# Turned token rows in DRAM: one array with 512 columns a block of features for each slot, in place of two halves of 256

## The chip, the cores and the metric

The kernel runs on one core of one Trainium2 chip. The metric is the device time of one execution in microseconds. A core has the engines TensorE (PE in the profile; its weight loads are PEld), VectorE (DVE), ScalarE (ACT), GpSimd (POOL) and SyncE (SP), and 16 DMA engines that serve the DMA queues of SP (q1 in the profile) and of POOL (q0).

## What is computed

Four batches of 1024 tokens with 1024 features go through a cross attention and a mixture of experts. Cut to what matters here:

```python
x = x + xattn(layernorm(x), ctx, Wq, bq, Wk, bk)      # x + teacher_logits @ softmax(q k^T)^T
xt = layernorm(x).reshape(4096, 1024)
scores = sigmoid(xt @ gate_w.T)
_, sel = top_k(scores + expert_bias, 2)               # 2 of 8 experts a token
order = argsort(sel.reshape(-1))                      # 8192 (token, expert) pairs, by expert
tok_idx = order // 2
routed_in = xt[tok_idx] * scores_sorted[:, None]
h = silu(ragged_dot(routed_in, w1t)) * ragged_dot(routed_in, w3t)   # hidden 704, bf16
routed_out = ragged_dot(h, w2t)
shared = (silu(xt @ sw1.T) * (xt @ sw3.T)) @ sw2.T    # float32, for every token
out = x + shared.at[tok_idx].add(routed_out)
```

## The kernel before

The work has three stages, and TensorE's order is written out by hand through all of them.

**Attention and routing** (to about 640 us). Tokens go through in tiles of 128. For each token tile the kernel also finds its two experts, scales its row by the two scores in bf16, and scatters the scaled rows (with the token's number behind the 1024 features) into a DRAM list `xrows`, one region an expert.

**Shared experts, and the turning of rows** (about 640 to 1473 us). Eight shared slots of 512 tokens in float32. A shared slot `s` is `up(s)` (L937: six blocks of products, the last five of them by a scheme of seven products over `xb`, `xs` and the weights) and two `down_pair` (L1033). `block(s + 1)` (L154) loads the next slot's 2 MB `xb` on SP's queue once the products of `up(s)` have read it; GpSimd makes the four sums `xs` of it (`differences`, L174); `residuals` (L996) loads the rows that `down_pair` adds to and stores. In slots 0 to 3 `convert` (L244) writes one more expert's weights as bf16 on POOL's queue.

In the same stage the generator `turns()` (L1001) prepares the first `NTURN` = 15 of the `NS` = 23 expert slots. An expert slot has 512 rows of one expert, in four quarters of 128. One step of the generator stands for one quarter: GpSimd gathers rows of a later quarter (`ask`, L1006, into one of four `xg` buffers), VectorE reads the token numbers from the gathered rows (L1022), SP turns the quarter with a DMA transpose into half of a tile `xh` (L1027; two such tiles), and after every second quarter SP stores `xh`, 128 partitions x 8 blocks of features x 256 columns, to DRAM (L1019, the last one L1031). `up(s)` calls the generator twice for each of its five blocks from s = 2 on (L974), so the steps are tied to TensorE's progress through the engines' program order. SP works its list in order: transposes, stores, `xb`, residuals and outputs stand in one queue.

**Expert slots** (1473 us to the end). For each of 23 slots (L1176) TensorE does 88 products (L131, `upwards`: 11 groups of 8 with weights `w13` stationary and the turned rows `xTb` moving; only as many columns as the slot has rows, 32 to 512), then the products of `w2` (L1161 to L1169). A slot's rows come from `fetch_turned(s)` (L906) for the first 15 slots and from `fetch_rows` (L882) with TensorE transposes for the rest; its weights come from gathers on POOL's queue, `fetch_up` (L888, `w13`, 22.5 KB a partition) and `fetch_down` (L897, `w2` with 10 KB a partition, and `w2t`). `w13` and `w2` are not fetched again where the expert stays the same two slots on. All of these have two buffers, by the slot's parity. When the 88 products of slot `s` are done, SP may issue `fetch_turned(s + 2)` (L1192) and GpSimd `fetch_up(s + 2)`; then come the four adds of slot `s`'s results into `out` (L1208, POOL's queue, DMAs that add in DRAM; GpSimd takes them in program order) and `fetch_down(s + 2)`. `fetch_turned(0)` and its weights are issued in the last shared slot (L1117), `fetch_turned(1)` after it (L1173).

The layout that the change touches is this: each slot's turned rows lie in DRAM as two tiles of [128, 8, 256] bf16, one for each half of 256 columns.

```python
xturned = [[dram.tile([P, KC, 2 * P], BF16, name=f"xturned_{i}_{h}") for h in range(2)]
           for i in range(NTURN)]
```

So a store writes 4 KB in one piece for each partition, and the load of a half, whose target `xTb` is [128, 8, 512], puts pieces of 256 columns (512 bytes) with gaps of as much between them.

Of the kernel before, what the change touches and what calls it, by code (L numbers as in the profile page):

```python
# [33 lines left out]
BF16 = mybir.dt.bfloat16  # L34
# [7 lines left out]
P = 128  # L42
# [6 lines left out]
KC = D // P  # L49
# [7 lines left out]
SLOT = 512  # L57
# [6 lines left out]
NTURN = 15  # L64
# [15 lines left out]
def xattn_moe_kernel(ctx: ExitStack, tc: tile.TileContext, x, ctxT, wqT, wkT, bqk, gwT, ebias,  # L80
                     w13, w2, w2t, sw13, sw2, sw2t, consts, out):
    nc = tc.nc

    dram = ctx.enter_context(tc.tile_pool(name="dram", bufs=1, space=DRAM))
# [10 lines left out]
    def const(k):  # L95
# [13 lines left out]
    width = cp.tile([P, NS, 1 + NQ], I32, name="width")  # L109
    beyond = cp.tile([P, NS, NQ], I32, name="beyond")  # L110
    tokens_of = [cp.tile([P, NQ], I32, name=f"toks_{i}") for i in range(NTURN)]
    xturned = [[dram.tile([P, KC, 2 * P], BF16, name=f"xturned_{i}_{h}") for h in range(2)]
               for i in range(NTURN)]


    places = bass_types.dram_disjoint_views(xrows, 2 * NT)
# [112 lines left out]
    with ExitStack() as a:  # L229
# [317 lines left out]
        with tc.manual_schedule(engines=vector_scalar):  # L547
# [37 lines left out]
            for p in range(NT // 2):  # L585
                g = 2 * p
                b, i = divmod(g, LT)
# [161 lines left out]
    def gather(dst, src, idx, **bound):  # L749
        nc.gpsimd.indirect_dma_start(out=dst, out_offset=None, in_=src,  # L750
                                     in_offset=bass.IndirectOffsetOnAxis(ap=idx, axis=0), **bound)
# [128 lines left out]
    weights, fetched, slots = [], {}, {}  # L880
# [22 lines left out]
    def xT_of(s):  # L903
        return bps[s % 2].tile([P, KC, SLOT], BF16, tag="xT", name=f"xTb_{s}")

    def fetch_turned(s):  # L906
        slots[s] = xT_of(s), tokens_of[s]
        for h in range(2):
            nc.sync.dma_start(slots[s][0][:, :, h * 2 * P : (h + 1) * 2 * P], xturned[s][h])

    def turned_rows(s, q):
        if q == 0:
# [19 lines left out]
    with shared, tc.manual_schedule(engines=vector_scalar | {mybir.EngineType.SP}):  # L932
# [68 lines left out]
        def turns():  # L1001

            blocks = list(itertools.product(range(NTURN), range(NQ)))
            asked = []

            def ask(s, q):  # L1006
                xg = tr.tile([P, ROW], BF16, tag="xg", name=f"xgt_{s}_{q}", bufs=4)
                gather(xg.bitcast(I32), xrows, li[:, s, q : q + 1])
                asked.append(xg)

            for b in blocks[:2]:
                ask(*b)
            yield
            done = None
            for j, (s, q) in enumerate(blocks):
                if j + 2 < len(blocks):
                    ask(*blocks[j + 2])
                if done:
                    nc.sync.dma_start(*done)  # L1019
                    done = None  # L1020
                xg = asked.pop(0)
                nc.vector.tensor_tensor(tokens_of[s][:, q : q + 1], xg[:, D : D + 2].bitcast(I32),  # L1022
                                        beyond[:, s, q : q + 1], ALU.bitwise_or)
                h, v = divmod(q, 2)
                if v == 0:
                    xh = tr.tile([P, KC, 2 * P], BF16, tag="xh", name=f"xh_{s}_{h}", bufs=2)
                nc.sync.dma_start_transpose(xh[:, :, v * P : (v + 1) * P], xg[:, :D])  # L1027
                if v:
                    done = xturned[s][h], xh
                yield  # L1030
            nc.sync.dma_start(*done)  # L1031

# [63 lines left out]
        tb = ExitStack()  # L1096
        table = tables(pool(tb, "tb", 1, "right"))
        turning = turns()
        residuals(0)
        for s in range(NJ):  # L1100
# [10 lines left out]
            if s + 1 == NJ:  # L1111
                for _ in turning:
                    pass
                tb.close()
                sums.close()
                bps.append(pool(ctx, "b0", 1, "right"))
                fetch_turned(0)  # L1117
                fetch_up(0)
                fetch_down(0)
                nextparts = list(widths(0))  # L1120
            else:
                block(s + 1)
# [48 lines left out]

    outs, adds = bass_types.dram_disjoint_views(out, NQ), []
    fetch_turned(1)  # L1173
    fetch_up(1)
    fetch_down(1)
    for s in range(NS):  # L1176
# [14 lines left out]
        if s + 2 < NTURN:  # L1191
            fetch_turned(s + 2)  # L1192
# [110 lines left out]
```

## Time and profile before

| | |
|---|---|
| Median of 3 runs | 2016.29 us (2012.39 to 2018.24) |
| The profiled execution's own time | 2016.26 us |
| Its span in the profile | 2014.5 us, mean granted TensorE clock 0.992 |
| Busy: PE, PEld, DVE, ACT, POOL | 97%, 58%, 41%, 26%, 32% |
| DMA moved | 340.37 MB in 179972 packets, mean 169 GB/s |
| POOL's queue q0, SP's queue q1 | 43024 packets, 172.78 MB; 136832 packets, 166.04 MB |
| Stores of turned rows (L1019, L1031) | 30, 512 KB each |
| Loads of turned rows (L909) | 30, 512 KB each |

Of a group of instructions the profile gives the line, engine, operation, names (target <- sources) and count, then the busy time and the mean ns of one, then the time that the engine idled before them and what ended most of that. A chain of waits is read in order of time: start, length, what ran or was waited for. A row of a table by stretches has the stretch and its length, then busy time (and instructions) of PE, PEld, DVE, ACT and POOL, the granted TensorE clock (1.00 is full), the share of the 16 DMA engines' time that packets took, and GB/s. A row of DMA queues has packets, MB and the share of the 16 engines' time in the stretch asked for. SPq means SP's DMA queue, where issues are seen.

### The profile page before, as it was taken

What the parts mean: (1) busy time and instruction counts of PE and PEld (TensorE: products, weight loads), DVE (VectorE), ACT (ScalarE), POOL (GpSimd) and SP (SyncE); (2) the same over time, 40 slices, a digit from 0 to 9 for tenths busy, and PEclk for the clock granted to TensorE, in tenths of its full rate; (3) what the DMA queues carried; (4) which work ended last, traced back from release to release, by engine and by line L of the source; (5) the groups of instructions that cost most, each with busy time, mean ns of one, the idle gap of its engine ahead of it and who ended that gap; (6) DMA issues with size and microseconds to landing.
All of it is one profiled execution on the core that took longest, in us unless ns stands there. A gap on an engine that the chain in (4) does not pass through costs nothing.

```text
span 2014.5 us, 24206 instructions
## 1 busy us (share of the span) xinstructions
PE 1961.7 (97%) x8992; PEld 1175.0 (58%) x9107; DVE 828.2 (41%) x2014; ACT 514.6 (26%) x900; POOL 650.2 (32%) x598
## 2 busy tenths in 40 slices
PE   8999999999999999999999999999999897999997
PEld 5555655655454448485858576767655553456665
DVE  5456566556863426313131313231333332224353
ACT  3344444454432101010101010101022232223232
POOL 0423433433642140312121212121124533256563
PEclk9999999999999999999999999999999998999999
DMA  4263473373765143595959272727646877489994
GB/s 122 85 172 116 150 197 117 119 209 135 243 204 210 64 114 98 149 221 138 211 141 239 84 204 80 194 90 188 237 99 127 247 194 226 102 216 334 297 306 81
DMA packets 179972, 340.37 MB, mean 169 GB/s; under 512 B 80400, under 2 KB 119824, under 8 KB 176016
## 3 DMA queue, kind: packets, MB, share of 16 engines
q0 software_dynamic: 43024, 172.78, 32.8%
q1 hardware_dynamic: 136832, 166.04, 27.0%
q8 instruction: 73, 1.20, 0.2%
q14 instruction: 43, 0.35, 0.1%
HBM read 280.80 MB, written 166.20 MB: 222 GB/s over the span
## 4 chain that ended last, share of the span: by engine, by line
PE 93%; DMA 3%; DVE 1%; issue 1%; ACT 0%; another core or an unknown queue 0%; POOL 0%; POOLq 0%; SPq 0%; DVEq 0%; ACTq 0%
PE pa L131 22%; PE bank L131 15%; PE pc L131 12%; PE bank L1169 6%; PE qa L131 6%; PE pb L131 6%; PE pu L131 4%; DMA xTb<-xturned 3%; PE pq L310 3%; PE qc L131 3%; PE pe L322 3%; PE pt_c L131 2%; PE pt_a L258 1%; PE qb L131 1%; PE pt_t L258 1%; PE pt_x L258 1%
## 5 line engine op out<-in xcount | busy, mean ns | idle before, releaser
L131 PE MATMUL bank<-xTb,w 128*128 128x0 bf16 x2024 | 318.9, 318 | 18.0 <-DMA xTb<-xturned 15.5
L131 PEld LDWEIGHTS <-w 128*128 128x128 bf16 x2024 | 190.8, 99 | 128.6 <-issue 22.7
L750 POOL DMA_INDIRECT xgt<-xrows,li x60 | 57.3, 955 | 431.8 <-DMA xh<-xgt 173.3
L1208 POOL DMA_INDIRECT out_dram<-yt,toks x92 | 146.7, 1595 | 115.7 <-DVE yt L1204 81.9
L1169 PE MATMUL bank<-w,hTb 128*128 128x0 bf16 x920 | 165.6, 327 | 3.1 <-DVE hTb L148 3.1
L275 POOL TENSOR_TENSOR rs<-ve,con 128x1 f32<-128x1 f32 x64 | 47.7, 745 | 321.7 <-DVE ve L273 318.0
L148 DVE TENSOR_TENSOR hTb<-sg_b,bank 128x512 bf16<-128x512 f32 x115 | 78.7, 687 | 162.7 <-PE bank L131 149.0
L131 PE MATMUL pa<-xs,sw_sb 128*128 128x256 f32 x560 | 132.3, 379 | 0.0
L1169 PEld LDWEIGHTS <-hTb 128*128 128x128 bf16 x920 | 72.2, 98 | 92.4 <-issue 13.7
L131 PE MATMUL pa<-aT,xT 128*128 128x512 f32 x256 | 116.8, 599 | 1.6 <-DVE x L412 1.4
L147 ACT ACTIVATE sg_b<-bank 128x512 f32<-128x512 f32 x115 | 68.4, 597 | 184.7 <-PE bank L131 158.7
L131 PEld LDWEIGHTS pa<-xs,sw_sb 128*128 128x128 f32 x560 | 106.4, 190 | 14.4
L1204 DVE COPY yt<-bank 128x512 f32<-128x512 f32 x92 | 61.6, 689 | 120.8 <-PE bank L1169 112.4
L1206 ACT COPY yt<-bank 128x512 f32<-128x512 f32 x92 | 53.5, 585 | 147.9 <-PE bank L1169 136.0
L964 DVE TENSOR_TENSOR one<-one,pb 128x256 f32<-128x256 f32 x35 | 14.7, 420 | 172.4 <-PE pb L131 172.4
L528 POOL DMA_INDIRECT xrows<-rr,toi x64 | 64.6, 1009 | 61.9 <-issue 40.1
L412 DVE SCALAR_TENSOR_TENSOR x<-pa,rs,x 128x512 f32<-128x512 f32 x64 | 47.8, 748 | 86.6 <-PE pa L131 80.6
L168 ACT ACTIVATE st_c<-pt_c 64x256 f32<-64x256 f32 x7 | 2.6, 377 | 311.8 <-PE pt_c L131 311.8
L1055 DVE TENSOR_TENSOR x2c<-x2c,qa 128x512 f32<-128x512 f32 x64 | 43.8, 685 | 93.5 <-PE qa L131 93.5
L268 DVE BATCH_NORM_STATS2 st<-x 128x6 f32<-128x512 f32 x128 | 81.8, 681 | 0.6
L750 POOL DMA_INDIRECT w<-w13b,wi x23 | 23.2, 1009 | 180.5 <-PE bank L131 152.7
L131 PE MATMUL pu<-xb,sw_sb 128*128 128x512 f32 x176 | 76.3, 594 | 0.9 <-PE pt_t L258 0.9
(268 smaller groups left out, 3445.0 us busy)
## 6 DMA issues: line engine op xcount, KB each, us to landing
w13b<-in_w_dram POOLq DMA_DIRECT2D x8, 2816.0 KB
x<-in_x_dram SPq DMA_DIRECT2D x32, 512.0 KB
x2d<-x SPq DMA_DIRECT2D x32, 512.0 KB
xtd<-xtT SPq DMA_DIRECT2D x32, 512.0 KB
xb<-xtd SPq DMA_DIRECT2D x8, 2048.0 KB
x2c<-x2d SPq DMA_DIRECT2D x16, 1024.0 KB
out_dram<-x2c SPq DMA_DIRECT2D x16, 1024.0 KB
xturned<-xh SPq DMA_DIRECT2D x30, 512.0 KB
```

Of the source, the lines that this page charges most:

```text
L131: nc.tensor.matmul(part(pp), w(c), part(xT(c)), start=start and c == 0, stop=c == blocks - 1, skip_group_check=not start)
L147: nc.scalar.activation(sg, pa, AF.Silu)
L148: nc.vector.tensor_tensor(hT[:, f, :], sg, pb, ALU.mult)
L258: nc.tensor.transpose(pt[:, j, :], src[:, c * P : (c + 1) * P], ident)
L268: nc.vector.bn_stats(st[:, h, :], src[:, h * 512 : (h + 1) * 512])
L310: nc.tensor.matmul(pq[:, i, j, :], w[c // CH][:, c % CH, :], ct[c // CH][:, c % CH, :], start=c == 0, stop=c == CC - 1)
L322: nc.tensor.matmul(pe[:, h, :], qs[b][:, m * P : (m + 1) * P], ks[b][:, h * 512 : (h + 1) * 512], start=True, stop=True)
L528: nc.gpsimd.indirect_dma_start(out=places[2 * (g + i) + k], out_offset=bass.IndirectOffsetOnAxis(ap=tois[k][:, i : i + 1], axis=0), in_=rr ...
L750: nc.gpsimd.indirect_dma_start(out=dst, out_offset=None, in_=src, in_offset=bass.IndirectOffsetOnAxis(ap=idx, axis=0), **bound)
L1169: nc.tensor.matmul(part(py), hT[:, f, toks], part(w[:, f, cols]), start=False, stop=f == NF - 1, skip_group_check=q < 2)
L1204: nc.vector.tensor_copy(yt[:, q, h * 512 : (h + 1) * 512], py)
L1208: adds.append([nc.gpsimd.indirect_dma_start(out=outs[q], out_offset=bass.IndirectOffsetOnAxis(ap=toks[:, q : q + 1], axis=0), in_=yt[:, q, ...
```

## The change

The two halves of a slot lie in one DRAM array, [128, 8, 512] bf16. A store still takes one tile `xh` of 256 columns, and its 256 columns of each block of features now lie as 512 bytes, with 512 bytes of the other half between them. The load of a slot is one DMA of 1 MB, with 8 KB in one piece for each partition on both sides, in place of two of 512 KB. The transposes, the gathers, the buffers in SBUF and their number, and what TensorE, VectorE, ScalarE and GpSimd do stay as they are.

```diff
-    xturned = [[dram.tile([P, KC, 2 * P], BF16, name=f"xturned_{i}_{h}") for h in range(2)]
-               for i in range(NTURN)]
+    xturned = [dram.tile([P, KC, SLOT], BF16, name=f"xturned_{i}") for i in range(NTURN)]
...
     def fetch_turned(s):
         slots[s] = xT_of(s), tokens_of[s]
-        for h in range(2):
-            nc.sync.dma_start(slots[s][0][:, :, h * 2 * P : (h + 1) * 2 * P], xturned[s][h])
+        nc.sync.dma_start(slots[s][0], xturned[s])
...
                 nc.sync.dma_start_transpose(xh[:, :, v * P : (v + 1) * P], xg[:, :D])
                 if v:
-                    done = xturned[s][h], xh
+                    done = xturned[s][:, :, h * 2 * P : (h + 1) * 2 * P], xh
                 yield
             nc.sync.dma_start(*done)
```

## The prediction

> **What bounds the kernel now.** I read the page first, then the waits of TensorE, then the chain, then what the DMA engines did inside the two stretches that the chain names. The page says that TensorE is the bound nearly everywhere, and its costliest group shows the one place where it is not:
>
> ```profile
> PE 1961.7 (97%) x8992; PEld 1175.0 (58%) x9107; DVE 828.2 (41%) x2014; ACT 514.6 (26%) x900; POOL 650.2 (32%) x598
> ...
> L131 PE MATMUL bank<-xTb,w 128*128 128x0 bf16 x2024 | 318.9, 318 | 18.0 <-DMA xTb<-xturned 15.5
> ```
>
> Of the 18.0 us that TensorE sat idle before the expert stage's first products, 15.5 ended when a load of turned rows landed. TensorE's waits between 1470 and 1820 us say how often:
>
> ```profile
> PE bank L131 <- DMA xTb<-xturned: 15.5, 2, 10.0
> ```
>
> Twice, once for 10.0 us. The chain (start, length, what) shows where; the timeline of TensorE gives the idle time in brackets:
>
> ```profile
> 1562.40 14.32 PE bank L131 x88
> ...
> 1577.30 30.70 DMA xTb<-xturned
> 1607.99 0.14 issue
> 1608.13 16.98 PE bank L131 x88
> ...
> 1632.95 14.32 PE bank L131 x88
> ...
> 1647.85 30.41 DMA xTb<-xturned
> 1678.26 0.14 issue
> 1678.40 20.69 PE bank L131 x88
> ```
>
> ```profile
> 1608.13 16.98 PE L131 MATMUL bank<-xTb,w 128*128 128x0 bf16 x88 [5.54 <-DMA xTb<-xturned]
> ```
>
> ```profile
> 1678.40 20.69 PE L131 MATMUL bank<-xTb,w 128*128 128x0 bf16 x88 [10.01 <-DMA xTb<-xturned]
> ```
>
> Counting the blocks of 88 from 1473.6 us, these are slots 6 and 9. Each follows a nearly empty slot (5 and 8), whose 88 products took 10.35 and 7.47 us, so less time than usual lay between issue and use. A load of 1 MB takes some 31 us here; beside a quiet POOL queue its 2048 packets pass in 4 us (1489.5 to 1493.5). Look also at the granted clock (the 0.50 or 1.00 behind POOL's column):
>
> ```profile
> 1608.00:1610.00 2.00, 1.87 (x6) 0.89 (x7) 0.00 (x0) 0.00 (x0) 1.69 (x3) 0.50 1.03 207
> 1614.00:1616.00 2.00, 2.00 (x14) 1.18 (x13) 0.69 (x1) 0.04 (x1) 0.00 (x0) 1.00 1.06 417
> 1678.00:1680.00 2.00, 1.60 (x4) 0.59 (x5) 0.00 (x0) 0.00 (x0) 1.06 (x2) 0.50 1.03 213
> ```
>
> After each wait TensorE runs at half clock for some microseconds. That is why slot 6's block took 16.98 us where slots 4 and 7 took 14.32, and slot 9's 20.69 where slots 10 to 12 took 18.99.
>
> Why is the load slow? The DMA view from 1582 to 1586 us, when expert weights (POOL's queue q0) and turned rows (SP's queue q1) are both waiting:
>
> ```profile
> q0 software_dynamic: 64, 1.44, 92.2%
> q1 hardware_dynamic: 64, 0.03, 2.7%
> ```
>
> Equal packet counts: the engines take one packet from each queue in turn. A weight packet is 1.44 MB / 64 = 22.5 KB and takes 0.922 x 64 us / 64 = 0.92 us; a packet of turned rows is 512 bytes and takes 27 ns. The load has 128 packets an engine, and each waits for one of q0's.
>
> **The change, part by part.** *The load.* Two DMAs of 1024 runs of 512 bytes become one DMA of 128 runs of 8 KB, or 8 packets an engine. From weight packets (0.92 us for 22.5 KB) or from the 4 KB rows of the stores (983.9 to 985.5 us: 0.864 x 25.6 us / 122 = 0.18 us) an 8 KB packet costs about 0.34 us, so 8 cost 2.7 us. Slot 6's load starts moving at 1578.1 and weights follow at 1579.9, so some five packets pass first and three wait for one of q0's each (3 x 0.92). It lands near 1584 us. Were each run cut into 4 KB pieces, some ten would wait, and it lands near 1591. TensorE wants it at 1602.4. Slot 9's load starts at 1648.6 and is wanted at 1668.4: the same sum gives 1654, or 1661. Both waits go.
>
> *What each is worth.* Slot 6: 5.54 idle + (16.98 - 14.32) half clock = 8.20 us. Slot 9: 10.01 + (20.69 - 18.99) = 11.71 us. Together 19.9 us.
>
> *What is late next.* For slot 6, the w13 packets end at 1588.0, 14 us early; the w2 packets at 1601.0, wanted at 1602.4 + 14.3 = 1616.7. Slot 7's w13 ends at 1608.7, and slot 7 now starts at 1624.6 instead of 1633. For slot 9, w13 ends at 1659.0, wanted at 1668.4, and everything before it comes 8.2 us sooner as well; it now lets at most eight packets of 0.34 us by, 2.7 us. Slot 14's load, which landed at 1814.5 for a start at 1815.8, gets margin too. Nothing else of TensorE's waits hangs on DMA in this stretch (2.3 us on VectorE, 0.4 on nothing visible), so later work moves up whole, and I count no second-order gain.
>
> *The store.* SBUF still holds 4 KB a partition, but the rows in DRAM are now cut into 512-byte runs 1 KB apart: 64 packets an engine instead of 8, for each of 30 stores. No row shows a 512-byte write to DRAM. From below: 64 x 27 ns = 1.7 us, the price of 512-byte reads, against 1.6 us now (983.9 to 985.5): nothing. A gain is excluded, since no byte less is written, in more packets. From above: 0.18 us each, as if a 4 KB packet cost its time whatever its size: 11.5 us, or 10 more a store. I take the low end: it is the same size between the same memories, and 4 KB rows show no difference by direction (0.16 to 0.18 us both ways). Here a rule speaks against the change: the Trainium skill, "DMA: Bandwidth & Descriptors", section Specifications, puts the smallest transfer at full rate at 512 bytes. By it the old load had nothing to gain, and the sum would be 0. By the rows, the 27 ns packet is 19 GB/s an engine against 24 for 22.5 KB (and its alternation with those is what costs). The rows decide, but the rule helps the store: 512-byte writes shouldn't fall off.
>
> The cover for the store is the turning stage (852 to 1416 us), in which TensorE never waits for data (one gap of 1.9 us at 1436). The turning's own slack: a gather lands at least 9 us before VectorE reads its token numbers (1067.4 and 1077.4, at the tightest), and the last transposes of a shared slot are over some 10 us before SP issues the next xb (1009.7 and 1020.2); GpSimd finishes the sums of xb at 1038.9, some 25 us before TensorE reads them. Behind a store on SP's queue lie the next transposes, xb and the residuals' loads. If weights are being converted (until 960.9 and 1066.0 us), a store alternates with packets of about 0.33 us: only what is left of a conversion can come between, a few us, under the same slack.
>
> *SP's issues.* A store's issue rises from 0.33 us to about 0.52, the price of the old load with as many runs: 30 x 0.2 us in 560, hidden. Fifteen load issues go. Slot 1's second half moves ahead of the last shared store on SP, 19 us earlier, with 38 to spare. Both versions wait once for the release of the xT buffer. The other engines' programs stay in the same order.
>
> *Sum.* The profiled execution took 2016.26 us, its span 2014.5 and 1.8 around it; the median of the three runs is 2016.29, so the sum stands for both: 2016.3 - 19.9 = 1996.4 us.
>
> **The rivals.** *A, both waits vanish* (my forecast): 1996.4, give or take 4 (the runs of before spread from 2012.4 to 2018.2). Chance 0.70.
>
> *B, only part of it comes.* Either one slot finds another input late (the lean slots 5 and 8 leave least time; then 2016.3 - 11.7 = 2004.6 or 2016.3 - 8.2 = 2008.1), or the half clock stays, since slot 13, as lean, lost the clock at 1811 us after only 2.5 us of idle time (15.6 gained, about 2000). For: the engines are full there, a share of 1.00 from 1577 to 1609. Against: the margins above. Middle 2004.6, chance 0.14.
>
> *C, the transfer comes no sooner.* If the engines are simply full, or the long runs aren't kept as long packets, the load still lands after about 30 us: 2016.3. Against: in the 25.7 us from slot 6's issue to its use the engines have only this to do on both queues: w13 8 x 0.92 = 7.4 us, slot 4's four adds about 8, w2 3.1, the load 2.7, together 21. Chance 0.09.
>
> *D, slower.* The 512-byte writes make the turning the bound: five stores lie in each 104 us shared slot, with 10 us to spare. With e us more a store, VectorE, which reads the gathered tokens in order with the evictions, stops TensorE by 5e - 10 in each of some six slots. That eats the 19.9 us at e = 2.7, or 4.3 us a store, 67 ns a packet, 2.5 times the read's price. At 90 ns (e = 4.2) it gives 2016.3 - 19.9 + 6 x 11 = 2062. For: writes with gaps are nowhere in the trace. Against: the row of equal size. Chance 0.07.
>
> **How the numbers follow.** About 0.3% (6 us) is what a measurement of this kernel can tell from no change. A and B are faster by more: 0.84. C is the same: 0.09. D is slower: 0.07. The range holds A with its spread and B: 1990 to 2008.5; C and D, 0.16, are left out.
>
> **What would show it.** Right: the group of xTb products loses its 15.5 us of DMA waits; blocks of slots 6 and 9 take 14.3 and 19.0 us at clock 1.00; xTb packets are of 8 KB and each load lands within 14 us; the turning stage ends where it did and TensorE stays full in it; the expert stage is 20 us shorter. Wrong: w13 or w2 named as the releaser before slot 6 or 9 (B); the chain still through xTb at 30 us (C); a VectorE wait for gathered rows, or TensorE idle between 860 and 1440 us (D).

## The result, and the profile after

| | before | after |
|---|---|---|
| Median | 2015.90 us of 4 runs (2012.39 to 2018.24) | 1989.92 us of 4 runs (1989.53 to 1991.77) |
| Profiled execution: own time, span | 2016.26, 2014.5 us | 1989.73, 1988.0 us |

The ratio is 0.9874 (95% interval 0.9857 to 0.9891): 26.0 us off, where the forecast was 19.9. In a later set of runs it was 0.9868 (0.9850 to 0.9885). The changed file is two lines shorter, so L131, L909 and L1169 of before are L130, L907 and L1167 here.

From the page of the changed kernel, the same two lines as before:

```profile
PE 1956.4 (98%) x8992; PEld 1174.0 (59%) x9107; DVE 827.9 (42%) x2014; ACT 514.5 (26%) x900; POOL 650.7 (33%) x598
...
L130 PE MATMUL bank<-xTb,w 128*128 128x0 bf16 x2024 | 313.9, 315 | 0.8 <-issue 0.5
```

TensorE's idle time before these products fell from 18.0 to 0.8 us. Its busy time fell too, from 318.9 to 313.9 us, with no product less: in slots 6 and 9, where the half clock after the waits is gone, it is 4.1 us less, and 1.0 in slot 19. TensorE's longest waits from 1470 us to the end (us in total, times, longest) name no load of turned rows at all:

```profile
PE ptb L918 <- PE bank L130: 0.7, 2, 0.4
PE bank L130 <- issue: 0.5, 1, 0.5
PE ptb L918 <- issue: 0.4, 2, 0.2
```

The chain through slots 5, 6, 7 and 9 is now only work of TensorE:

```profile
1587.44 10.20 PE bank L130 x88
...
1605.49 14.31 PE bank L130 x88
...
1627.64 14.31 PE bank L130 x88
...
1662.66 19.00 PE bank L130 x88
```

Slot 6 takes 14.31 us (before 16.98), slot 9 takes 19.00 (before 20.69), and no `DMA xTb` stands between. In the stretch in which slot 9's products begin, the granted clock (behind POOL's column) is 1.00, where before it was 0.50:

```profile
1662.00:1664.00 2.00, 2.00 (x32) 1.19 (x31) 1.89 (x3) 1.07 (x2) 0.00 (x0) 1.00 1.07 423
```

The DMA queues while slot 6's load passes, from 1581 to 1585 us (packets, MB, share of the engines' time):

```profile
q1 hardware_dynamic: 134, 0.97, 62.2%
q0 software_dynamic: 31, 0.70, 40.9%
```

Of the 134 packets of SP's queue 118 are the load's (0.97 MB / 8 KB). The packet records have all 128 between 1580.6 and 1584.2 us, median 309 ns, mean 369; the first weight packet came at 1583.5, when seven of an engine's eight had passed. From its first packet to its last the load takes 3.6 us; before, with 2048 packets of 512 bytes, 28.2 us.

In the turning stage TensorE is as full as before. This is the stretch from 864 to 1416 us in the changed kernel:

```profile
864.00:1416.00 552.00, 552.00 (x2082) 384.59 (x2081) 150.93 (x366) 59.86 (x154) 103.49 (x82) 1.00 0.62 161
```

**Where the 26.5 us of the span went.** From the start of each slot's products in both traces: slot 5 to slot 7 is 8.20 us shorter, slot 8 to slot 10 is 12.12. Those are the two places of the forecast. Three more differences are outside it: slot 0 begins 2.89 us later, slot 13 to 14 is 4.72 us shorter, and slot 19 to 20 is 3.79 us shorter; small ones make the remaining 0.6. The experiments had to say what these are, and whether the whole gain lies in the load.

### The profile page after: what moved, and what is told of

Read it like the earlier page. It is cut to its first block, busy times and chain, and to the rows that moved or that the text cites. A ratio compares the mean times of both kernels' runs of the same rounds, so it can differ in the third digit from the quotient of the medians.

```text
span 1988.0 us, 24188 instructions
## 1 busy us (share of the span) xinstructions
PE 1956.4 (98%) x8992; PEld 1174.0 (59%) x9107; DVE 827.9 (42%) x2014; ACT 514.5 (26%) x900; POOL 650.7 (33%) x598
## 3 DMA queue, kind: packets, MB, share of 16 engines
q1 hardware_dynamic: 134672, 166.04, 26.8%
## 4 chain that ended last, share of the span: by engine, by line
PE 96%; DVE 1%; issue 1%; POOL 0%; ACT 0%; DMA 0%; POOLq 0%; DVEq 0%; SPq 0%; ACTq 0%
PE pa L130 23%; PE bank L130 15%; PE pc L130 12%; PE bank L1167 8%; PE qa L130 6%; PE pb L130 6%; PE pu L130 4%; PE pq L309 3%; PE qc L130 3%; PE pe L321 3%; PE pt_c L130 2%; PE pt_a L257 1%; PE qb L130 1%; PE pt_t L257 1%; PE pt_x L257 1%
## 5 line engine op out<-in xcount | busy, mean ns | idle before, releaser
L130 PE MATMUL bank<-xTb,w 128*128 128x0 bf16 x2024 | 313.9, 315 | 0.8 <-issue 0.5
L130 PEld LDWEIGHTS <-w 128*128 128x128 bf16 x2024 | 188.3, 98 | 109.0 <-issue 1.0
L1167 PE MATMUL bank<-w,hTb 128*128 128x0 bf16 x920 | 163.2, 325 | 0.0
L130 PE MATMUL pa<-xs,sw_sb 128*128 128x256 f32 x560 | 132.3, 379 | 0.0
L1167 PEld LDWEIGHTS <-hTb 128*128 128x128 bf16 x920 | 72.0, 97 | 85.9 <-issue 9.9
L130 PE MATMUL pa<-aT,xT 128*128 128x512 f32 x256 | 116.8, 599 | 1.5 <-DVE x L411 1.4
L130 PEld LDWEIGHTS pa<-xs,sw_sb 128*128 128x128 f32 x560 | 106.6, 190 | 14.3
L130 PE MATMUL pu<-xb,sw_sb 128*128 128x512 f32 x176 | 78.0, 604 | 0.9 <-PE pt_t L257 0.9
L130 PEld LDWEIGHTS pa<-aT,xT 128*128 128x128 f32 x256 | 46.3, 190 | 48.8 <-issue 47.8
```

The lines of the kernel that those rows point to most:

```text
L130: nc.tensor.matmul(part(pp), w(c), part(xT(c)), start=start and c == 0, stop=c == blocks - 1, skip_group_check=not start)
L1167: nc.tensor.matmul(part(py), hT[:, f, toks], part(w[:, f, cols]), start=False, stop=f == NF - 1, skip_group_check=q < 2)
```

## The experiments

The first four ran together, beside 15 runs of the kernel before (median 2013.91 us, 2011.33 to 2017.12), the last three together beside 19 (2015.38 us, 2011.18 to 2018.91). Unless it says otherwise, a kernel differs from the changed one only in `fetch_turned`.

**before_again: the kernel before, profiled a second time.** Is what differed outside slots 6 and 9 the change, or the chance of one execution?

> The kernel before, unchanged, profiled once more. The change gained 26.0 us where 19.9 were forecast; in the two traces, 20.3 us of it come in slots 6 and 9, 4.7 more in slot 13 and 4.0 in slots 18 and 19, and 2.9 are given back before slot 0. Theory 1 (the rest is a matter of the execution: half-clock spells of TensorE that fall on lean slots or not): the waits of 5.5 and 10.0 us for turned rows come again within 1 us, but the half-clock spells outside them (1811, 1931 us) lie elsewhere or are missing, and slots 13 and 19 take other times than before. Theory 2 (the rest belongs to the layout): slots 13 and 19 lose the same 4.7 and 4.0 us again.

It took 2016.58 us in its one run, nearly the same time as the first profile, made up differently. The waits of TensorE from 1470 us, and its timeline at slot 14 (start, us; idle before and releaser in brackets):

```profile
PE bank L131 <- DMA xTb<-xturned: 20.7, 3, 10.4
```

```profile
1819.22 5.10 PE L131 MATMUL bank<-xTb,w 128*128 128x0 bf16 x22 [4.12 <-DMA xTb<-xturned]
```

There is a third wait, at slot 14, 4.12 us long, and slot 14's block then takes 17.16 us (15.80 in the first profile), with a half-clock spell of 3.4 us at its start. The chain goes through it:

```profile
1790.97 28.11 DMA xTb<-xturned
...
1819.22 8.03 PE bank L131 x40
```

From issue to landing slot 14's load takes 28 us, nearly as long as the others (some 31). In the first profile its packets ended at 1814.5, but slot 13 had a stall of its own just before; the chain of the first profile at that place has:

```profile
1796.63 7.62 PE bank L131 x72
...
1804.30 4.32 another core or an unknown queue
```

These 4.3 us, and a half-clock spell at 1811 us, stood where the wait would have stood. What held ScalarE there, for whose results slot 13's products of `w2` waited, is not in the trace, and none of the other eight traces has this stall. From slot 13 to slot 15 the two executions of before take 43.24 and 44.16 us, the changed kernel 38.52: both lost the time, one to the wait, the other to a stall that covered it. The other two differences belong to single executions and not to the change: here slot 19 to 20 takes 11.30 us (15.00 in the first profile, with a half-clock spell at 1931 us; 11.21 after), and the half-clock spells at 630 and 1440 us that delay slot 0 in the changed kernel are here as well. Against this execution the changed kernel gains 8.93 us from slot 5 to 7, 12.13 from 8 to 10, and 5.64 from 13 to 15: 26.7 of the 26.8 us between these two spans (2014.8 and 1988.0).

**store_only: the new array, with the load left in 512-byte runs.**

```diff
-        nc.sync.dma_start(slots[s][0], xturned[s])
+        for h in range(2):
+            cols = slice(h * 2 * P, (h + 1) * 2 * P)
+            nc.sync.dma_start(slots[s][0][:, :, cols], xturned[s][:, :, cols])
```

> The new array in DRAM with its stores of 512-byte runs, but loaded as before in two halves of 512-byte runs: the cost of the stores alone. If the gain is all in the load and the stores are hidden: 2012 to 2019 us, with the two waits for turned rows as before (5.5 and 10.0 us), and TensorE full from 864 to 1416 us. If the stores cost time by themselves: above 2020. If something else in the new array gains (one array instead of two): below 2006.

It took 2015.49 us (2014.32 to 2017.45), ratio 1.0008 (1.0000 to 1.0017). All three waits for turned rows are there:

```profile
PE bank L130 <- DMA xTb<-xturned: 20.9, 3, 10.7
```

and TensorE is busy for 552.00 of the 552 us from 864 to 1416. By the interval the 512-byte stores cost at most 0.17%, some 3 us, and the new array by itself brings nothing: the gain lies in the load. What a 512-byte write costs can be read in the changed kernel's DMA view from 874 to 878 us, in which a store passes:

```profile
q1 hardware_dynamic: 2177, 0.94, 98.5%
```

0.985 x 4 us x 16 engines / 2177 = 29 ns a packet, transposes among them; this store's own 1024 records have a mean of 27.0 ns. Over the other stores of 512-byte runs the mean goes up to 35 ns, and the median of all is 27.

**load_1k: eight DMAs of 1 KB runs (64 packets an engine), and load_256: four of 256-byte runs (256 an engine).** If what counts is the number of packets, the first should stand between the kernels and the second be slower than before; if bytes or the array's layout count, neither.

```diff
+        for c in range(KC):
+            nc.sync.dma_start(slots[s][0][:, c, :], xturned[s][:, c, :])
```

> The new array, loaded as 8 DMAs of one block of features each, in runs of 1 KB: 64 packets an engine instead of 128 or 8. If packets of the two queues alternate one for one, some 40 pass before the weights come and 24 wait for 8 packets of w13 and 16 of the adds: slot 6's load lands some 15 us after its issue (31 before, 7 after), before TensorE wants it, and the time is that of the changed kernel, 1988 to 1994 us. If the bytes of full engines set the landing, it lands after 30 us as before and the time is 2012 to 2019.

```diff
+        for q in range(NQ):
+            cols = slice(q * P, (q + 1) * P)
+            nc.sync.dma_start(slots[s][0][:, :, cols], xturned[s][:, :, cols])
```

> The new array, loaded as 4 DMAs of 128 columns each, in runs of 256 bytes: 256 packets an engine. If packets alternate, about 105 pass before the weights come and 150 wait for one packet each of w13, the adds, w2 and the next w13, so slot 6's load lands 40 us or more after its issue and slots 6 and 9 wait at least 10 us longer each: 2035 to 2070 us. If the bytes set the landing, the same as the kernel before, 2012 to 2019 us.

load_1k took 1995.37 us (1992.74 to 1998.31), ratio 0.9900 (0.9880 to 0.9921). The load of slots 6 and 9 takes 22.9 us, slot 14's 26.0, where some 15 were expected, and the time is 1.4 us above what was expected: a miss. The chain at slot 9 shows why. SP's queue is named SPq; its issues follow each other, and the last begins only at 1645.5:

```profile
1642.02 0.32 SPq L908
...
1644.28 0.66 SPq L908
...
1644.98 0.51 SPq L908
...
1645.54 22.23 DMA xTb<-xturned
...
1667.81 19.33 PE bank L130 x81
```

Eight issues took 4.0 us, and the first weight packet came at 1644.3, 1.3 us after the load's first. Only 13 of the 64 packets an engine had passed by then, where 40 were expected, and 16 at 1646; the other 48 then passed beside 54 of POOL's queue. In the DMA view from 1645 to 1649 us they do so, one for one:

```profile
q0 software_dynamic: 64, 1.44, 86.6%
q1 hardware_dynamic: 60, 0.06, 4.3%
```

The alternation holds as expected; the head start had been counted too large. The loads of slots 9 and 14 still come too late, so three short waits remain, of 0.3 and 3.0 us inside slot 9's products and 1.9 us inside slot 14's, and one half-clock spell in slot 9.

load_256 took 2056.87 us (2054.60 to 2057.05), ratio 1.0208 (1.0191 to 1.0225): slower than before by 43.0 us, with the same bytes. Its loads take 40.0 us (slot 6), 38.2 (slot 9) and 45.7 (slot 14). TensorE's waits from 1470 us:

```profile
PE bank L130 <- DMA xTb<-xturned: 38.4, 2, 20.6
PE bank L130 <- issue: 23.4, 2, 22.9
```

The 22.9 us on "issue" are slot 14's wait: its products begin at 1855.8, and its last packets end at 1855.2. The queues from 1590 to 1594 us, while slot 6's load passes:

```profile
q0 software_dynamic: 201, 0.76, 95.0%
q1 hardware_dynamic: 201, 0.05, 9.9%
```

Equal counts again, a 256-byte packet (0.099 x 64 us / 201 = 32 ns in this stretch) for each row of POOL's queue (0.76 MB / 201 = 3.8 KB, 0.30 us). SP's four issues for slot 6 took far longer than those for slot 5, which found its queue empty:

```profile
1553.48 3.11 SPq L909 DMA_DIRECT2D xTb<-xturned  x4
...
1575.63 24.59 SPq L909 DMA_DIRECT2D xTb<-xturned  x4
```

The fourth alone took 22.3 us, while packets of the first three were still to pass. So in slots 6, 9 and 14 this kernel has a burden that the others' loads of these slots haven't, and how much of its time is due to that isn't shown; that the queues alternate is what the counts show. In order of packets an engine, slot 6's load and the kernel's time are: 8: 3.6 us, 1989.92; 64: 22.9 us, 1995.37; 128: 28.2 us, 2013.91 to 2015.90; 256: 40.0 us, 2056.87. The step from 128 to 64 is small because the packets that pass ahead of the weights are fewer too: 60 of 128 an engine before, 13 of 64 here.

**only_6_9, only_14 and after_again: which slots the gain belongs to.** The 8 KB load only where `s in (6, 9)`, or only where `s == 14` (the same edit with that condition), with two loads of 512-byte runs everywhere else; and the changed kernel once more.

```diff
+        if s in (6, 9):
+            nc.sync.dma_start(slots[s][0], xturned[s])
+            return
+        for h in range(2):
+            cols = slice(h * 2 * P, (h + 1) * 2 * P)
+            nc.sync.dma_start(slots[s][0][:, :, cols], xturned[s][:, :, cols])
```

> The new array, but only the slots 6 and 9 are loaded in runs of 8 KB, all others in two halves of 512-byte runs. In the traces so far these two slots are worth 8.2 or 8.9 and 12.1 us. If the rest of the gain is a third wait, that of slot 14, which the profiled execution of before hid behind a half-clock spell: 1991 to 1996 us, 3 to 7 us over the changed kernel, with slot 14 still waiting about 4 us for its rows. If the rest comes from something all loads share or from chance: the same as the changed kernel within 1.5 us.

> The new array, but only slot 14 is loaded in runs of 8 KB, all others in two halves of 512-byte runs. If slot 14's load is a third wait: 4.7 to 7.6 us less than the kernel before (the traces with 512-byte loads lose that much from slot 13's start to slot 15's), so 2006 to 2011 us, with the waits of slots 6 and 9 left as they are. If it is not: the time of the kernel before, 2012 to 2016 us.

> The changed kernel once more, beside the other two. 1988 to 1992 us, no wait of TensorE for turned rows, half-clock spells before slot 0 in some executions and not in others.

| | median of runs | ratio (95%) | gain |
|---|---|---|---|
| only_6_9 | 1996.19 us of 5 | 0.9913 (0.9898 to 0.9928) | 19.2 us |
| only_14 | 2009.93 us of 14 | 0.9977 (0.9968 to 0.9986) | 5.4 us |
| after_again | 1988.53 us of 4 | 0.9868 (0.9850 to 0.9885) | 26.9 us |

only_6_9 is the forecast made into a kernel: 19.2 us gained and 1996.19 us, where the forecast said 19.9 and 1996.4. Slot 14 still waits in it. Its timeline at that place:

```profile
1796.34 4.85 PE L130 MATMUL bank<-xTb,w 128*128 128x0 bf16 x20 [4.14 <-DMA xg<-xrows,li]
```

The releaser named is a gather that landed at 1796.3, whose rows only the transposes at 1804.3 read; slot 14's turned rows passed from 1768.8 to 1795.4, 26.6 us as before. Two transfers ended within 1 us, and the profile names the later. In only_14 the two waits of the forecast stay, and the third is gone:

```profile
PE bank L130 <- DMA xTb<-xturned: 15.6, 2, 10.6
```

The parts make 24.6 us of 26.9. The 2.2 us between (0.0110 of the time against 0.0132) lie within the three intervals taken together (0.0015 and 0.0009 of the parts, 0.0018 of the whole), and the runs don't say whether they are more than that. only_6_9 came out 0.2 us above what was expected of it; the other two lie within.

## Why the prediction was right, and which step was mis-sized

- *What bounds the kernel there.* Right. The group lost its waits, slots 6 and 9 run at full clock in 14.31 and 19.00 us, and they gave 8.20 and 12.12 us in the profiled pair, where 8.20 and 11.71 were summed. As a kernel of their own, only_6_9, they gave 19.2 us, where 19.9 were forecast.
- *Why the load is slow.* Right, and now shown by the series of loads: with equal bytes, more packets make it slower, and at 60 to 64 and 201 to 201 the queues alternate. Equal counts could also come of long bursts in turn; in the records of before from 1582 to 1586 us each of the 64 small packets starts within 4 ns of the end of a different weight packet, so the turn is one packet. Not each of the 128 packets waits for one, as was written: before, 60 an engine had passed when the first weight packet came at 1579.9. The packet of 8 KB was estimated at 0.34 us; its median was 0.309, its mean 0.369. The load was put at some 6 us (1578.1 to 1584) and took 3.6, since seven packets an engine passed ahead of the weights and not five. The case of 4 KB pieces was summed wrongly: by its own figures (1.8 us at 0.18 us each) ten of sixteen would have passed and six waited, so some 1586 us and not 1591. Nothing hung on it.
- *The store.* Right: the low end of 27 ns was taken, the median is 27, and store_only shows the stage hiding it. Rival D, which began at 67 ns, falls.
- *The rule of the Trainium skill* ("DMA: Bandwidth & Descriptors", Specifications: full rate from 512 bytes) would have made the sum 0. The measurement decides: 26.0 us. The rule speaks of a rate. In rate the two loads differ, 19 GB/s an engine at 27 ns and 26.5 at 309, but beside a quiet POOL queue the old load passed in 4 us; what cost was the turn that a packet had to wait for. The 512-byte writes go at the rate of the reads, as the prediction took from the rule, and that too is under the 26.5 of the long rows.
- *What is late next.* This step failed in size. It put slot 14 among what "gets margin too", at no gain, since the trace showed the load's last packet 1.3 us before its products began. That was hardly a margin: in before_again, store_only and only_6_9, where slot 14 waits, its products begin 0.9 us after the last packet. And it was chance that TensorE was not waiting: a stall at slot 13 in that one execution covered a third wait of 4.1 us and the half clock behind it, worth 5.4 us by only_14. Slot 13, which goes before it, is nearly empty as slots 5 and 8 are, so slot 14's load of 26.7 us had as little time as those of slots 6 and 9: from issue to use 24.5 us in the changed kernel, against 25.7 and 20.5. The step looked at what was idle in one trace and not at how long the load took against the time it had.
- *Rivals B and C.* Nothing else was late: neither `w13` nor `w2` is named before slots 6 and 9, the clock at both is full, and the load came after 3.6 us. Both fall.
- *Sum.* 19.9 forecast; 26.0 measured; 5.4 of the 6.1 between are the third wait. The measured 1989.92 us is 6.5 us under the forecast, beyond the 4 that rival A allowed, and 0.1 below the low end of the range, 1990: the direction and the mechanism were right, the range was too narrow on that side for want of this term.

## What to carry to other kernels

Where a queue of long rows is busy (here 4 to 22.5 KB), a load's time is about the number of packets that it still has to move when those rows come, by the time of one of those rows, whatever its bytes: lay data that is needed soon in DRAM so that the load has few, long runs, and let the short runs fall on the side that has cover, here the store. Before counting a slow transfer that "lands just in time" as free, ask what held the engine back at that place, and look at a second execution. The half clock after a wait belongs to its price: here (2.66 + 1.70) of the 19.9 us at slots 6 and 9.

## What was not expected of the hardware

- The same program in nearly the same time (2016.26 and 2016.58 us) had two waits for turned rows in one execution and three in the other.
- A 512-byte write to DRAM took 27 ns at the median, the same as a 512-byte read.
- An issue on SP costs more with more runs, and far more when earlier packets are still to pass. One of 128 runs of 8 KB took 0.32 us; one of 1024 runs of 512 bytes took 0.52 or 0.67 us for slots 5 and 6; four of 1024 runs of 256 bytes took 3.1 us for slot 5 and 24.6 us for slot 6. The kernel before has such a hold too, of 9.6 us at the second issue for slot 7, but slot 7 didn't need its rows so soon.
